# Sorting the edges of a graph layer by a scatter through DRAM in place of permutation products

## Chip, cores, metric

One core of one Trainium2 chip. The metric is the device time of one execution in microseconds (us); the kernel before takes 2326.83 us (median of 3 runs, 2326.06 to 2328.2).

## What is computed

Four graph layers, each `x = x + layer(relu(layernorm(x)))`, on `x` of 128 batches x 64 nodes x 256 features, all in float32. Layer 0 is a two-product network with batch norms around a normalised adjacency matrix; layer 1 works in the eigenvectors of the graph's Laplacian; layer 2 (the third) is two graph convolutions followed by LSTMs over windows of nodes; layer 3 (the fourth) is attention along 512 edges:

```
# layer 2, the convolutions
h = relu(einsum('ts,bsh->bth', adj, x @ Wg0 + bg0))
h = relu(einsum('ts,bsh->bth', adj, h @ Wg1 + bg1))
# ... LSTMs over windows of 1, 2, 3 and 4 nodes

# layer 3, E = 512 edges from src[e] to dst[e]
Xq, Xv = H @ W_lin.T, H @ W_val.T            # split into 4 heads
e = einsum('behd,hd->beh', leaky_relu(Xq[:, src] + Xq[:, dst], 0.2), a)
e = e + log(A0[src, dst] + 1e-8)
attn = softmax of e over the edges of the same src
Y = segment_sum(attn * Xv[:, dst], src)
out = Y @ W_out.T
```

Layer 3 is a sum over edges, so the edges may be taken in any order. The kernel sorts them by `src`, so that edges of one source stand side by side.

## The kernel before

The node features are kept in SBUF as 16 blocks `X[0..15]` of 512 rows (8 batches). TensorE (PE) does the products, VectorE (DVE) and ScalarE (ACT) take results out of PSUM, SyncE (SP) issues all DMAs, GpSimd (POOL) makes a few constants and otherwise does nothing. A float32 product of 128x512 is two entries of about 0.43 us each in the trace.

**The convolutions of layer 2** (`layer2`, L2088) run over the 16 blocks. `block(i)` (L2115) issues, in this order: the product with the first weights (`ps<-a,w`, four 128x512 products), taken out by DVE as `g`; the second mixing by the adjacency matrix of the block before (`features(i - 1)`, `ps<-BDA,y`), taken out by ACT into `big`; the first mixing of the block after (`mixed(i + 1)`, `ps<-BDA,h`), taken out as `a`, half by DVE and half by ACT; the product with the second weights (`pt<-w,g`), taken out by DVE in two halves as `y`; and the layer norm of block `i + 2` (`normed`), on DVE (`n_st`, `n_mv`, `n_v`, `n_r`, `n_m`) and ACT (`n_y`, `h`), with a DMA of `X[i + 2]` to DRAM (`xs<-X`). The LSTMs (`windows`, L2145) follow; their weights are loaded over blocks of `X` that are no longer needed, and their first inputs (`ls_tx`) are prepared ahead of time on DVE.

**The edge tables** of layer 3 (`edges`, L2332) are built inside layer 2, at the head of `block(2)`. Three small DMAs bring `src` and `dst` as columns (`ed_ci`, L2341: edge 128 c + p on partition p) and `src` as a row on all partitions (`ed_cmp`, L2342); POOL makes the index rows `ed_J`, `ed_C`, `ed_P` (L2348). With `key = src * 512 + e`, the place of an edge is the number of smaller keys: for each of four columns of edges DVE compares the row of all keys with 128 keys (`ed_cmp`) and sums (`ed_rank`). Then, for each column, DVE writes a 128x512 matrix with a one at each edge's place (`ed_perm`), and PE multiplies it with `src` and with `dst`: eight products `pe<-ed_perm,ed_col` into two PSUM banks. DVE copies the two sorted rows out (`ed_s`). Everything else follows from these two rows: the one-hot matrices of the ends `OS` and `OD` (again in buffers named `ed_perm`), their sum `ed_S`, their transposes `ed_OST` and `ed_ODT` (eight PE transposes `pe<-ident,ed_perm`), the marks of edges that continue a source (`ed_cont`, `ed_contr`), and the logarithm of the edge weights (`ed_log`: products `pe<-ed_perm,A` and `pe<-ed_cmp,ones`, and a Ln on ACT, which loads another function table). The buffers named `ed_` that are not used later lie in a pool `l3e`, which is given back when the tables are done.

**The order of instructions.** In layer 2 a scheduler of the framework orders the instructions of each engine by their dependences; each engine works through its list strictly in order. `nc.hold(nc.mark())` around `edges` puts each of its PE, DVE and ACT operations behind the last one issued so far on the same engine; where behind it, the scheduler decides. The trace attributes all PE, DVE and ACT operations to a helper's line, L799, so they are told apart here by the names of their tiles.

Of the kernel before, what the change touches and what calls it, by code (L numbers as in the profile page):

```python
# [8 lines left out]
F32 = mybir.dt.float32  # L9
I32 = mybir.dt.int32  # L10
AF = mybir.ActivationFunctionType
ALU = mybir.AluOpType
# [1453 lines left out]
class Kernel:  # L1466
# [621 lines left out]
    def layer2(self, pool, psum, ps2, ps0):  # L2088

        nc, o = self.nc, self.o  # L2090
        W0, W1, b1, N0 = self.tables2
        hs, as_, ys = {}, {}, {}

        def normed(i):
            if i < NB:
                hs[i] = self.norm(pool, i)
                nc.sync.dma_start(self.spilled(i), self.X[i][:])

        def mixed(i):
            if i < NB:  # L2100
                a = as_[i] = pool.tile([P, 2, BT], F32, name="a")
                self.mix(psum, hs.pop(i), self.BDA, lambda dc, p: self.move(a[:, dc, :], p[:]))

        def features(i):
            v = self.nodes(i // 4)
            b = 8 * (i % 4)
            self.mix(psum, ys.pop(i), self.BDA, lambda dc, p: self.act(
                v[:, dc, :, b:b + 8].rearrange("p n b -> p b n"), p[:].rearrange("p (b n) -> p b n", n=N), AF.Relu))

        def begin():  # L2110
            normed(0)
            mixed(0)
            normed(1)

        def block(i):  # L2115
            if i == 2:
                with ExitStack() as ce:
                    epool = ce.enter_context(self.tc.tile_pool(name="l3e", bufs=1, side="right"))
                    nc.hold(nc.mark())
                    self.edges(self.w3, epool, ps0)  # L2120
                    nc.hold()
            a = as_.pop(i)
            g = pool.tile([P, 2, BT], F32, name="g")
            for hc in range(2):
                p = psum.tile([P, BT], F32, name="ps")
                for kc in range(2):
                    self.mm(p[:], W0[:, kc, hc * P:(hc + 1) * P], a[:, kc, :], kc == 0, kc == 1)
                o.tt(g[:, hc, :].rearrange("p (b n) -> p b n", n=N), p[:].rearrange("p (b n) -> p b n", n=N),
                     N0[:, hc, None, :].to_broadcast([P, BT // N, N]), ALU.max)
            if i:  # L2130
                features(i - 1)
            mixed(i + 1)
            y = ys[i] = pool.tile([P, TPB, D], F32, name="y")
            for jj in range(0, TPB, 2):
                p = ps2.tile([P, 2, D], F32, name="pt")
                for j in range(2):
                    for kc in range(2):
                        self.mm(p[:, j, :], g[:, kc, (jj + j) * P:(jj + j + 1) * P], W1[:, kc, :],
                                kc == 0, kc == 1)
                o.add(y[:, jj:jj + 2, :], p[:], b1[:, None, :].to_broadcast([P, 2, D]))  # L2140
            normed(i + 2)

        return [begin] + [lambda i=i: block(i) for i in range(NB)] + [lambda: features(NB - 1)]
# [188 lines left out]
    def edges(self, w, pool, psum):  # L2332


        nc, o, io = self.nc, self.o, self.io
        ci, cmp = pool.tile([P, 2, 4], I32, name="ed_ci"), pool.tile([P, E], F32, name="ed_cmp")
        ri = cmp[:].bitcast(I32)
        with nc.allow_non_contiguous_dma("a few values"):
            for x, n in enumerate(("src", "dst")):
                a = io["L3_gnn_" + n]  # L2340
                nc.sync.dma_start(ci[:, x, :], a.rearrange("(c p) -> p c", p=P))  # L2341
        nc.sync.dma_start(ri, io["L3_gnn_src"].partition_broadcast(P))  # L2342
        row, col = pool.tile([P, E], F32, name="ed_row"), pool.tile([P, 2, 4], F32, name="ed_col")
        o.copy(row[:], ri)
        o.copy(col[:], ci[:])
        J, C = pool.tile([P, E], F32, name="ed_J"), pool.tile([P, 4], F32, name="ed_C")
        Pm = pool.tile([P, 1], F32, name="ed_P")
        iota = lambda t, pat, m: nc.gpsimd.iota(t[:], pattern=pat, base=0, channel_multiplier=m,  # L2348
                                                allow_small_or_imprecise_dtypes=True)
        iota(J, [[1, E]], 0)  # L2350
        iota(C, [[P, 4]], 1)
        iota(Pm, [[0, 1]], 1)
        up = pool.tile([P, 1], F32, name="ed_up")
        o.ts(up[:], Pm[:], float(N), ALU.is_ge, -float(N), ALU.mult)
        o.add(Pm[:], Pm[:], up[:])

        o.stt(row[:], row[:], float(E), J[:], ALU.mult, ALU.add)
        key = pool.tile([P, 4], F32, name="ed_key")
        o.stt(key[:], col[:, 0, :], float(E), C[:], ALU.mult, ALU.add)
        rank = pool.tile([P, 4], F32, name="ed_rank")  # L2360
        ps = [psum.tile([P, E], F32, name="pe") for x in range(2)]
        for c in range(4):
            o.ts(cmp[:], row[:], key[:, c:c + 1], ALU.is_lt)
            o.red(rank[:, c:c + 1], cmp[:], ALU.add)
            perm = pool.tile([P, E], F32, name="ed_perm", bufs=2)
            o.ts(perm[:], J[:], rank[:, c:c + 1], ALU.is_equal)
            for x in range(2):
                self.mm(ps[x][:], col[:, x, c:c + 1].to_broadcast([P, P]), perm[:], c == 0, c == 3)
        srt = []
        for x in range(2):  # L2370
            s = pool.tile([P, E], F32, name=f"ed_s{x}")
            o.copy(s[:], ps[x][:])
            srt.append(s)
        self.OS, self.OD = (pool.tile([P, E], F32, name="ed_perm", bufs=2) for _ in range(2))
        self.S2 = w.tile([P, E], F32, name="ed_S2")
        o.ts(self.OS[:], srt[0][:], Pm[:], ALU.is_equal)
        o.ts(self.OD[:], srt[1][:], Pm[:], ALU.is_equal)
        o.add(self.S2[:], self.OS[:], self.OD[:])
        self.OST, self.ODT = (w.tile([P, 4, N], F32, name="ed_" + n) for n in ("OST", "ODT"))
        for a, y in ((self.OS, self.OST), (self.OD, self.ODT)):  # L2380
            p = psum.tile([P, 4, N], F32, name="pe")
            for c in range(4):
                nc.tensor.transpose(p[:, c, :], a[:N, c * P:(c + 1) * P], self.ident[:N, :N])
            o.copy(y[:], p[:])

        self.cont, self.contr = (w.tile([P, E], F32, name="ed_" + n) for n in ("cont", "contr"))
        nc.vector.memset(self.cont[:], 0.0)
        nc.vector.memset(self.contr[:], 0.0)
        o.tt(self.cont[:, 1:E], srt[0][:, 1:E], srt[0][:, 0:E - 1], ALU.is_equal)
        o.copy(self.contr[:, 0:E - 1], self.cont[:, 1:E])  # L2390

        p = psum.tile([P, E], F32, name="pe")
        self.mm(p[:N, :], self.A[:], self.OS[:N, :])
        ga = cmp[:N, :]
        o.mul(ga, p[:N, :], self.OD[:N, :])
        p = psum.tile([P, E], F32, name="pe")
        self.mm(p[0:1, :], self.ones[:N, 0:1], ga)
        self.logA = w.tile([1, E], F32, name="ed_log")
        eps = pool.tile([1, 1], F32, name="ed_eps")
        nc.vector.memset(eps[:], 1e-8)  # L2400
        self.act(self.logA[:], p[0:1, :], AF.Ln, bias=eps[:])

        ac = self.columns(pool, "ed_ac", io["L3_gnn_a"].rearrange("h d -> (h d)"))
        self.apad = w.tile([P, 2, P], F32, name="ed_apad")
        nc.vector.memset(self.apad[:], 0.0)
        for fc in range(2):
            for x in range(2):
                s = slice(64 * x, 64 * x + 64)
                o.ts(self.apad[s, fc, 64 + 2 * fc + x:64 + 2 * fc + x + 1], ac[s, fc:fc + 1], 0.8, ALU.mult)
# [321 lines left out]
    def run(self):  # L2731
        self.begin()
        dram = self.ctx.enter_context(self.tc.tile_pool(name="xs", bufs=1, space=bass.MemoryType.DRAM))
        self.xs = dram.tile([B * N, D], F32, name="xs")
        cx, pools = self.stage([(f"big{q}", 1) for q in range(NG)])
        with cx:
            self.big = [pool.tile([P, 2, 4 * BT], F32, name="big") for pool in pools]
            with ExitStack() as ex:
                self.consts1 = ex.enter_context(self.tc.tile_pool(name="l1c", bufs=1))
                self.eigenvectors()  # L2740
                self.layers12()
            self.windows()
        self.layer3()
# [43 lines left out]
```

## Time and profile before

| | |
|---|---|
| median of 3 runs | 2326.83 us |
| profiled execution, its own time | 2326.85 us |
| profiled execution, span from first to last instruction | 2325.1 us |
| granted TensorE clock, mean | 0.997 |
| PE busy | 2283.6 us (98%) |
| DVE busy | 1629.3 us (70%) |
| ACT busy | 1139.5 us (49%) |
| POOL busy | 3.0 us |
| layer 2's 16 blocks, PE | 504.6 to 680.6 us of the span |
| edge tables, DVE | 513.3 to 536.2 us of the span |

The profile is of one execution. "Busy" is the time in which an engine had an instruction under way; matmuls are pipelined, so a busy PE is not one at its peak. The timeline gives, for each group of like instructions in order, its start and length; the start of the next group less its own start is the PE time that it took. Of several products in a row each entry overlaps the next.

### The profile page before, as it was taken

To read this page: it belongs to the slowest core of one execution; us is meant where nothing else is said; L and a number is where in the kernel's file an instruction comes from. 1 tells how busy PE (TensorE), PEld (TensorE's weight loads), DVE (VectorE), ACT (ScalarE), POOL (GpSimd) and SP (SyncE) were. 2 spreads that over 40 slices of the span, in tenths; PEclk is the share of its full clock that TensorE was granted. 3 is DMA by queue.
4 is the path that set the end of the run, shared out by engine and by line. 5 is a ranking of instruction groups with operands and counts; after the bars stand their busy time and mean duration, and the time that the engine had idled before them with its cause. 6 is when DMAs were issued, how large, how long until landed. Compare 5 with 4: busy or idle time off the path is not lost.

```text
span 2325.1 us, 32725 instructions
## 1 busy us (share of the span) xinstructions
PE 2283.6 (98%) x12169; PEld 1633.1 (70%) x12169; DVE 1629.3 (70%) x4054; ACT 1139.5 (49%) x2483; POOL 3.0 (0%) x26
## 2 busy tenths in 40 slices
PE   7999998999999999999999999999999999999999
PEld 4554445676777788888999998888885544554544
DVE  8887676888447777666767676559756686766667
ACT  5765865754436654433444444336435544444321
POOL 0000000000000000000000000000000000000000
PEclk9999999999999999999999999999999999999999
DMA  5000211230000000001000002000010000000001
GB/s 171 1 1 26 65 56 30 71 83 19 1 37 0 1 19 1 1 1 37 1 1 1 1 1 73 1 1 17 1 46 28 1 5 15 15 19 14 14 24 46
DMA packets 61065, 54.81 MB, mean 24 GB/s; under 512 B 15203, under 2 KB 58724, under 8 KB 60900
## 3 DMA queue, kind: packets, MB, share of 16 engines
q1 hardware_dynamic: 60900, 52.66, 7.4%
q8 instruction: 97, 1.59, 0.3%
q14 instruction: 68, 0.56, 0.1%
HBM read 35.86 MB, written 16.78 MB: 23 GB/s over the span
## 4 chain that ended last, share of the span: by engine, by line
PE 79%; DVE 3%; issue 1%; ACT 1%; DMA 0%; SPq 0%; ACTq 0%; DVEq 0%
PE ps L799 69%; PE acc L799 5%; PE pt L799 4%; PE pe L799 1%; PE y L799 1%; DVE aw L799 1%; DVE X L799 1%; DVE sm_m L799 0%; DVE XV L799 0%; ACT ls_g L799 0%; ACT h L799 0%; DVE ls_g L799 0%; ACT big L799 0%; DVE ls_t L799 0%; DVE sm_e L799 0%
## 5 line engine op out<-in xcount | busy, mean ns | idle before, releaser
L799 ACT ACTIVATE ls_g<-ls_g,ls_b 128x512 f32<-128x512 f32 (+4 forms) x472 | 243.1, 565 | 151.4 <-DVE ls_g L799 149.6
L799 ACT ACTIVATE ls_g<-ps,ls_b 128x256 f32<-128x256 f32 (+3 forms) x268 | 115.5, 470 | 330.9 <-PE ps L799 327.7
L799 PE MATMUL ps<-z,w 128*128 128x512 f32 x512 | 254.9, 621 | 0.9 <-ACT z L799 0.9
L799 PE MATMUL ps<-big,X 128*128 128x176 f32 (+3 forms) x848 | 212.7, 366 | 0.1
L799 DVE TENSOR_TENSOR ls_g<-ls_z,ps 128x512 f32<-128x512 f32 (+5 forms) x256 | 146.8, 579 | 91.9 <-PE ps L799 90.4
L799 DVE TENSOR_TENSOR aw<-at,ed_OST 128x1024 f32<-128x1024 f32 x128 | 149.9, 1219 | 83.0 <-PE ps L799 82.8
L799 PE MATMUL ps<-ls_tx,X 128*128 128x160 f32 (+2 forms) x960 | 206.8, 326 | 0.6 <-ACT ls_g L799 0.6
L799 PE MATMUL ps<-X,X 128*128 128x160 f32 (+1 forms) x896 | 199.1, 306 | 0.0
L799 PE MATMUL ps<-X,ls_w 128*128 128x256 f32 x640 | 190.5, 379 | 0.0
L799 PEld LDWEIGHTS ps<-ls_tx,X 128*128 128x128 f32 x960 | 161.8, 190 | 15.1 <-DVE X L799 4.8
L799 PEld LDWEIGHTS ps<-big,X 128*128 128x128 f32 x848 | 145.9, 190 | 29.7 <-issue 19.4
L799 DVE TENSOR_TENSOR X<-ls_g 128x1024 f32<-128x1024 f32 (+2 forms) x108 | 117.4, 1087 | 49.9 <-ACT ls_g L799 49.8
L799 ACT ACTIVATE r<-ps 128x512 f32<-128x512 f32 x256 | 131.6, 614 | 41.5 <-PE ps L799 41.4
L799 PEld LDWEIGHTS ps<-X,X 128*128 128x128 f32 x896 | 148.4, 190 | 0.0
L799 PE MATMUL ps<-X,ls_s 128*128 128x256 f32 x480 | 142.3, 379 | 0.0
L799 PEld LDWEIGHTS ps<-z,w 128*128 128x128 f32 x512 | 87.2, 190 | 69.0 <-issue 60.2
L799 PE MATMUL ps<-ls_tx,ls_s 128*128 128x256 f32 x464 | 134.8, 379 | 0.0
L799 PE MATMUL ps<-ed_S,Q 64*128 64x512 f32 x512 | 132.9, 618 | 1.4 <-DVE hT L799 0.7
L799 PE MATMUL ps<-ls_tx,ls_w 128*128 128x256 f32 x464 | 133.2, 380 | 0.0
L799 PEld LDWEIGHTS ps<-X,ls_w 128*128 128x128 f32 x640 | 121.4, 190 | 16.8 <-DVE X L799 0.3
L799 PE MATMUL ps<-big,ls_w 128*128 128x256 f32 x464 | 131.9, 379 | 0.7 <-ACT ls_z L799 0.7
L799 PE MATMUL ps<-aw,ed_ODT 128*64 128x512 f32 x512 | 117.3, 595 | 0.1
(545 smaller groups left out, 4019.0 us busy)
## 6 DMA issues: line engine op xcount, KB each, us to landing
X<-in_x_dram SPq DMA_DIRECT2D x32, 512.0 KB
xs<-X SPq DMA_DIRECT2D x16, 512.0 KB
X<-xs SPq DMA_DIRECT2D x16, 512.0 KB
out_dram<-X SPq DMA_DIRECT2D x31, 256.0 KB
X<-in_L_gnn_Wih_t_dram SPq DMA_DIRECT2D x4, 512.0 KB
ls_w<-in_L_gnn_Wih_t_dram SPq DMA_DIRECT2D x4, 512.0 KB
ls_w<-in_L_gnn_Whh_t_dram SPq DMA_DIRECT2D x4, 512.0 KB
w<-in_L_gnn_W_t_dram SPq DMA_DIRECT2D x2, 512.0 KB
```

What stands on the lines that cost most here:

```text
L799: i = method(*a, **kw)
```

## The change

The sort is done by DMA. DVE turns the four rank columns into integers (`ed_at`). POOL then issues, for each column and each end, an indirect DMA that writes 128 integers of `ed_ci` to the places `ed_at` of a DRAM tensor `ends[x]` (8 DMAs), and two plain DMAs that bring `ends[0]` and `ends[1]` back as rows on all 128 partitions. The permutation matrices, their eight PE products and their two PSUM buffers are gone; DVE's copies `ed_s` convert the integers of the returned rows to float32. The work is cut in two: the first part (loads, ranks, DMAs) is issued at the head of `block(4)`, the second (`sorted`, from the two rows to the tables) at the head of `block(9)`, each with its own `hold`. The pool `l3e` stays open from one to the other.

```diff
         def block(i):
-            if i == 2:
-                with ExitStack() as ce:
-                    epool = ce.enter_context(self.tc.tile_pool(name="l3e", bufs=1, side="right"))
-                    nc.hold(nc.mark())
-                    self.edges(self.w3, epool, ps0)
-                    nc.hold()
+            if i == 4:
+                self.ce = ExitStack()
+                epool = self.ce.enter_context(self.tc.tile_pool(name="l3e", bufs=1, side="right"))
+                nc.hold(nc.mark())
+                self.tables3 = self.edges(self.w3, epool, ps0)
+                nc.hold()
+            if i == 9:
+                nc.hold(nc.mark())
+                self.tables3()
+                nc.hold()
+                self.ce.close()
...
         rank = pool.tile([P, 4], F32, name="ed_rank")
-        ps = [psum.tile([P, E], F32, name="pe") for x in range(2)]
+        at = pool.tile([P, 4], I32, name="ed_at")
         for c in range(4):
             o.ts(cmp[:], row[:], key[:, c:c + 1], ALU.is_lt)
             o.red(rank[:, c:c + 1], cmp[:], ALU.add)
-            perm = pool.tile([P, E], F32, name="ed_perm", bufs=2)
-            o.ts(perm[:], J[:], rank[:, c:c + 1], ALU.is_equal)
-            for x in range(2):
-                self.mm(ps[x][:], col[:, x, c:c + 1].to_broadcast([P, P]), perm[:], c == 0, c == 3)
+        o.copy(at[:], rank[:])
+
         srt = []
         for x in range(2):
-            s = pool.tile([P, E], F32, name=f"ed_s{x}")
-            o.copy(s[:], ps[x][:])
-            srt.append(s)
+            for c in range(4):
+                nc.gpsimd.indirect_dma_start(self.ends[x][:], bass.IndirectOffsetOnAxis(ap=at[:, c:c + 1], axis=0),
+                                             ci[:, x, c:c + 1], None)
+            s = pool.tile([P, E], F32, name="ed_perm", bufs=2)[:].bitcast(I32)
+            nc.gpsimd.dma_start(s, self.ends[x][:].rearrange("e o -> (o e)").partition_broadcast(P))
+            srt.append((pool.tile([P, E], F32, name=f"ed_s{x}"), s))
+        return lambda: self.sorted(w, pool, psum, Pm, cmp, *srt)
+
+    def sorted(self, w, pool, psum, Pm, cmp, *srt):
+
+        nc, o, io = self.nc, self.o, self.io
+        for x, s in srt:
+            o.copy(x[:], s)
+        srt = [x for x, s in srt]
         self.OS, self.OD = (pool.tile([P, E], F32, name="ed_perm", bufs=2) for _ in range(2))
...
         self.xs = dram.tile([B * N, D], F32, name="xs")
+        self.ends = [dram.tile([E, 1], I32, name=f"ends{x}") for x in range(2)]
```

## The prediction, on record before the changed kernel ran

> **What bounds the kernel now.** First the head of the page, then the chain of waits over the stretch in which the edge tables are built, because a share over the whole span does not say who sets the pace there.
>
> ```profile
> span 2325.1 us, 32725 instructions
> PE 2283.6 (98%) x12169; PEld 1633.1 (70%) x12169; DVE 1629.3 (70%) x4054; ACT 1139.5 (49%) x2483; POOL 3.0 (0%) x26
> ```
>
> The chain of waits from 500 to 600 us (start, length, what):
>
> ```profile
> 513.55 7.00 PE ps L799 x40
> 520.55 3.46 PE pt L799 x16
> 524.01 6.87 PE pe L799 x16
> 530.87 0.86 PE ps L799 x2
> 531.73 0.39 PE pe L799 x4
> 532.12 1.91 PE ps L799 x4
> 534.04 1.39 PE pe L799 x6
> 535.43 1.50 PE ps L799 x6
> 536.93 0.95 PE pe L799 x2
> 537.88 3.32 PE ps L799 x28
> 541.20 3.46 PE pt L799 x16
> 544.65 7.00 PE ps L799 x40
> 551.66 3.46 PE pt L799 x16
> 555.11 7.00 PE ps L799 x40
> ```
>
> The chain is PE and nothing else. A block of layer 2 costs 7.00 + 3.46 = 10.46 us, the same beside the table work and far from it. The `pe` entries are the tables' own products, put between: 6.87 us for the sixteen entries of the permutation products, then 0.39, 1.39 and 0.95 us. Now the other engines, by windows (PE busy, PEld, DVE, ACT, POOL, clock, DMA share, GB/s):
>
> ```profile
> 528.00:532.00 4.00, 4.00 (x13) 1.65 (x11) 4.00 (x22) 1.59 (x4) 0.00 (x0) 1.00 0.45 131
> 590.00:600.00 10.00, 10.00 (x56) 7.90 (x55) 4.72 (x15) 4.73 (x8) 0.00 (x0) 1.00 0.01 2
> ```
>
> DVE is full during the table work and half empty at 590 us; PE is full in both. So the permutation products are real time on the engine that sets the end, and DVE work here is not.
>
> **What the Trainium skill says.** "DMA: Bandwidth & Descriptors", section "Anatomy of one DMA — SWDGE (gpsimd) path", prices a DMA issued from GpSimd at about 2.0 us fixed plus bytes/436e3 us, most of the fixed part being the wait until the last byte has landed. The same page, "Latency and other measured facts", gives about 1 us to the first byte for such a DMA and 0.6 us from SyncE. The trace before has no DMA from POOL at all; its nearest rows are the two 16 KB loads at the start, from SP:
>
> ```profile
> 0.74 0.58 SPq L1509 DMA_DIRECT2D A<-in_adj_dram  x1
> 1.38 0.58 SPq L1510 DMA_DIRECT2D AT<-in_adj_t_dram  x1
> 2.88 0.21 DVE L799 TENSOR_REDUCE f_a_rs<-A 64x1 f32<-64x64 f32 x1 [1.23 <-DMA A<-in_adj_dram]
> 3.62 0.21 DVE L799 TENSOR_REDUCE f_a_cs<-AT 64x1 f32<-64x64 f32 x1 [0.53 <-DMA AT<-in_adj_t_dram]
> ```
>
> From issue to first use 2.88 - 0.74 = 2.14 us and 3.62 - 1.38 = 2.24 us, which agrees with the fixed price. "SBUF — State Buffer", its box on the "DVE blocks DMA" trap, adds that DVE operations in a two-port mode keep GpSimd from writing descriptors: a DMA of 620 ns took 3100 ns there. No run here shows that yet.
>
> **The change, part by part.**
>
> *Removed from PE:* eight products, sixteen entries, 6.87 us from the chain (523.84 to 530.71 in the timeline). No stall is hidden in it: 16 x 0.43 = 6.9. All of it lies on the path.
>
> *Moved on PE:* the eight transposes, the product with `A` and the one with `ones`, from block 2 to the start of block 9. Before they took 0.39 + 0.39 + 1.00 + 0.95 = 2.73 us, and cut the neighbours into pieces: the `ps` entries around them sum to 0.86 + 1.91 + 1.50 + 3.32 = 7.59 us instead of 7.00, so 0.59. Check: 544.65 - 524.01 = 20.64 = 10.46 + 6.87 + 2.73 + 0.59, to rounding. In the changed instruction order the transposes stand together, then one 128x512 product, `A`, one product, `ones`, and the block goes on; `ps<-BDA,y`, split before (1.99 us in place of 1.78), stays whole, a gain of 0.2. Against that, `ones` now has one product of 0.86 us ahead of it to cover DVE's `ed_cmp` (683 ns and its signals, after the product with `A` has drained). I estimate 0 to 1 us of PE wait and take 0.3. Net on PE: 6.87 + 0.2 - 0.3 = 6.8 us.
>
> *DVE:* four `ed_perm` operations go (371 to 477 ns, 1.8 us) and two PSUM copies of 0.68 us become two conversions in SBUF (nearest row: the 0.41 us cast of `ed_row`); one small copy of 0.16 us is added. Some 2.2 us less, and the rest is spread over blocks 1 to 9. Taken as nothing, because PE never waited in the fuller version. *ACT:* one of two 1.28 us table loads goes, as no `n_y` follows `ed_log` any more; nothing, ACT being half idle. The six `ls_tx` subtractions move from block 4 to block 9, since they use memory of `l3e`; their first reader stands at 681.5 us, more than 70 us later: nothing. *SP:* the same DMAs in the same order; the new ones pass none of them.
>
> *Added: a chain of DMAs on POOL.* Ten DMAs go into POOL's queue, empty after the three index rows. Each scatter waits for the scatter two before it (same DRAM tensor), and each read-back for its tensor's last scatter. Two chains run interleaved, so five links deep if POOL issues fast, ten if each DMA in effect waits for the one before. A link costs at least 2.2 us (the SP rows), 2.6 with the 0.4 us that the skill puts on GpSimd's first byte; computing 128 destinations in software makes it more. I take 3.5 us, an estimate that leaves 0.9 us for it; the upper bound adds the lock's 3.1 - 0.6 = 2.5 us: 6.0. So the chain takes 5 x 3.5 = 17.5 us likely, 5 x 2.2 = 11 us at least, 10 x 3.5 = 35 us if serial, 10 x 6.0 = 60 us at worst.
>
> *The added wait.* DVE's first `ed_s` copy waits for the first row read back. Behind it in DVE's list are the second `y` of block 5 and everything after; PE's `ps<-BDA,y` in block 6 waits for that `y`. The window: the blocks start on PE at 523.84 (block 2), 534.30, 544.76, 555.22 (block 5). `ed_at` follows block 2's second `g`, about 4 us after that block's start (517.12 against 513.38 for block 1), with 0.6 us for the operation: about 528.5. The first `ed_s` follows block 5's first `y`, 9.1 us after the start (522.49 against 513.38), plus 0.6: 564.9. Window 36.4 us. PE still has a second-weights half and block 6's first products, so it starves only some 3 us later: 39 us.
>
> **Sum:** 2326.85 us of the profiled execution (span 2325.1 and 1.75 around it; equal to the median of 2326.83 to 0.02) - 6.8 = 2320.05 us. From block 10 on all engines have the same order as before, and PE fills the boundary to the LSTMs without a gap, so the shift should reach the end.
>
> **Rivals.** *The main case* (gain kept): 0.77, time 2318.8 to 2321.8.
>
> *The chain is somewhat late*, 41 to 46 us of DMA: PE waits 2 to 7 us in block 6, the gain shrinks to 5 to 0 us, time 2322 to 2327. For: the price of computed destinations is not in the trace, and the first use of that path may be dearer. Against: it needs links of 8 us and more in two chains, or over 4 us in one. 0.09.
>
> *The wait exceeds what was removed*, at DVE's first `ed_s`. At 39 + 6.8 = 46 us of chain the change breaks even; from there each microsecond is one lost. At the worst, 60 us: 2326.85 - 6.8 + 21 = 2341 us. It decides at links of 4.6 us in one serial chain, or 9.2 us in two. For: the lock of the shared port and descriptors for single integers. Against: DVE's operations at 530 to 565 us are under 0.7 us each and mostly read PSUM, so that ten locks in a row are unlikely. 0.08.
>
> *The products were not what PE waited for*: if DVE had set the pace at 513 to 536 us, the removal would bring only DVE's 2.2 us: 2324.6. Against it stands the chain without a DVE piece. 0.04; and 0.02 for a larger gain.
>
> **How the numbers follow.** A measurement of this kernel can tell about 0.2%, 4.65 us, from no change. Faster than 2322.2 us: the main case, the larger gain, and 0.02 of the late one: 0.81. Slower than 2331.5 us: 0.07 of the 0.08 above. Within: the other 0.07 of the late case, the 2324.6 us case, and 0.01: 0.12. The time is that of the main case, 2320.1. The range, 2318.7 to 2324.7, takes in the main case, the case without PE's wait and the nearer half of the late one: 0.77 + 0.04 + 0.04 = 0.85.
>
> **What would show it.** Right: no `pe<-ed_perm,ed_col`; block starts on PE 10.46 us apart from block 2 to 9; the last scatter landed before 555 us; no idle time of DVE before `ed_s`; block 9 longer by about 3.2 us; the first `ps<-big,X` at about 673.8 us instead of 680.6. Wrong: DVE idle before `ed_s` until a DMA, with PE idle in block 6, or an LSTM start that moved less than PE's removed time.

## The result, and the profile after

The changed kernel takes 2322.21 us (median of 20 runs), the kernel before, run beside it on the same chip, 2328.57 us (20 runs). The ratio is 0.9974, with a 95% interval of 0.9967 to 0.9981: 6.1 us less (4.4 to 7.7). Forecast were 2320.1 us and 6.8 us less.

The head of the page, and its line for the new DMA queue (packets, MB, share):

```profile
span 2316.7 us, 32710 instructions
PE 2274.4 (98%) x12153; PEld 1628.0 (70%) x12153; DVE 1626.7 (70%) x4051; ACT 1138.3 (49%) x2482; POOL 12.0 (1%) x36
q0 software_dynamic: 416, 0.53, 0.1%
```

PE has 16 entries fewer, DVE three operations, ACT one (the table load); POOL has ten DMAs more and is still idle for 99% of the span. The chain of waits over the same stretch as before, and on to the new place of the tables:

```profile
513.42 7.00 PE ps L799 x40
520.42 3.46 PE pt L799 x16
523.88 7.00 PE ps L799 x40
530.88 3.46 PE pt L799 x16
...
593.64 3.46 PE pt L799 x16
597.10 0.64 PE pe L799 x8
597.74 1.06 PE ps L799 x2
598.79 1.00 PE pe L799 x2
599.79 1.06 PE ps L799 x2
600.85 0.95 PE pe L799 x2
601.80 5.49 PE ps L799 x36
```

Where 6.87 us of `pe` stood, the next block follows at once, and the blocks from 513 to 597 us are 10.46 us each. What is left of the tables on PE stands at 597 us in three pieces. The chain holds nothing but PE: no piece of DMA, POOL or DVE has come in. The two windows shown of before (PE busy, PEld, DVE, ACT, POOL, clock, DMA share, GB/s):

```profile
528.00:532.00 4.00, 4.00 (x32) 3.86 (x32) 4.00 (x22) 2.92 (x6) 2.35 (x3) 1.00 0.01 0
590.00:600.00 10.00, 10.00 (x62) 7.67 (x61) 4.90 (x17) 5.27 (x9) 0.00 (x0) 1.00 0.01 2
```

From 528 to 532 us PE is as full as it was, but with 32 entries of a block in place of 13 that were mostly permutation products. DVE is full as before, and POOL now works beside it.

The executions of one kernel differ by several microseconds in their first 500 us, before anything that the change touches. So the traces are compared by a distance: from the first product of block 1 (`ps<-a,w`) to the first product of the LSTMs (`ps<-big,X`), both on PE. It holds all that was removed, moved or added:

| kernel | block 1 | LSTMs | distance, us | less than before |
|---|---|---|---|---|
| before | 513.38 | 680.62 | 167.24 | |
| after | 513.25 | 673.49 | 160.24 | 7.00 |

The two profiled spans differ by 8.4 us. The other 1.4 us come from elsewhere: at the start of layer 3 the execution shown of before ran at a granted clock of 0.50 from 1745.4 to 1752.2 us, and one group of eight products took 3.78 us there; after has a clock of 1.00 and 1.99 us for the same group. Of the experiments' traces, some show the long form (x1: 3.78 us) and some the short one (x3: 1.99 us), with or without the change. It is no part of the change.

The DMAs on POOL, and their reader (timelines of POOL and DVE; start, length, idle time before and what ended it):

```profile
528.43 1.14 POOL L2375 DMA_INDIRECT ends<-ed_ci,ed_at  x1 [155.62 <-DVE n_r L799]
529.87 0.99 POOL L2375 DMA_INDIRECT ends<-ed_ci,ed_at  x1 [0.30 <-issue]
531.78 0.96 POOL L2375 DMA_INDIRECT ends<-ed_ci,ed_at  x1 [0.92 <-DMA ends<-ed_ci,ed_at]
...
541.31 0.58 POOL L2378 DMA_DIRECT2D ed_perm<-ends  x1 [0.25 <-issue]
544.28 0.56 POOL L2378 DMA_DIRECT2D ed_perm<-ends  x1 [2.40 <-DMA ends<-ed_ci,ed_at]
```

```profile
565.76 0.16 DVE L799 SCALAR_TENSOR_TENSOR n_m<-n_mv,n_r 128x4 f32<-128x4 f32 x1
565.85 0.42 DVE L799 CAST ed_s<-ed_perm 128x512 f32<-128x512 int32 x1
566.18 0.68 DVE L799 TENSOR_TENSOR y<-pt,w_b 128x512 f32<-128x512 f32 x1
```

The trace has the landing of four of the eight scatters: 2.5 to 4.3 us from issue (median 3.2 us). A read-back takes 4.0 us. The first and third scatter go to different places of one tensor, and the third waits for the first. The second row has landed at 544.28 + 4.0 = 548.3 us. DVE comes to `ed_s` at 565.85 us, without idle time in front of it: 17.5 us to spare.

### The profile page after: what moved, and what is told of

Same layout as the page of the kernel before. It is cut to its first block, busy times and chain, and to the rows that moved or that the text cites. A ratio compares the mean times of both kernels' runs of the same rounds, so it can differ in the third digit from the quotient of the medians.

```text
span 2316.7 us, 32710 instructions
## 1 busy us (share of the span) xinstructions
PE 2274.4 (98%) x12153; PEld 1628.0 (70%) x12153; DVE 1626.7 (70%) x4051; ACT 1138.3 (49%) x2482; POOL 12.0 (1%) x36
## 4 chain that ended last, share of the span: by engine, by line
PE 79%; DVE 3%; ACT 1%; issue 1%; DMA 0%; SPq 0%; ACTq 0%; DVEq 0%
PE ps L799 69%; PE acc L799 5%; PE pt L799 4%; PE y L799 1%; PE pe L799 1%; DVE aw L799 1%; DVE X L799 1%; DVE sm_m L799 0%; DVE XV L799 0%; ACT ls_g L799 0%; ACT h L799 0%; DVE ls_g L799 0%; DMA X<-in_L_gnn_Wih_t_dram 0%; ACT big L799 0%; DVE ls_t L799 0%
## 5 line engine op out<-in xcount | busy, mean ns | idle before, releaser
L799 ACT ACTIVATE big<-ps 128x512 f32<-128x512 f32 x96 | 69.2, 751 | 102.9 <-PE ps L799 101.6
```

Source lines behind the costliest of these rows:

```text
L799: i = method(*a, **kw)
```

## Experiments

Two theories stood against each other at first. **Theory:** the gain is the PE time of the removed products, and the DMA chain is free because five blocks of other work stand between its issue and its reader. **Rivals:** the gain comes from the new places of the two parts; or the DMA chain costs something that hides part of the gain. Each run is read by the distance above and by its ratio to the kernel before (with a 95% interval). Where an expectation names the start of the LSTMs in us of one execution (x1, x3, x5, x6), it is read as a distance too: 673.5 us stands for 160.24, 680.6 for 167.24.

### The products kept, the new places used

```diff
-            nc.gpsimd.indirect_dma_start(self.ends[x][:], ...)   # 8, and the two read-backs
     def sorted(...):
+            o.ts(perm[:], J[:], rank[:, c:c + 1], ALU.is_equal)   # 4
+                self.mm(ps[x][:], col[:, x, c:c + 1].to_broadcast([P, P]), perm[:], c == 0, c == 3)   # 8
+            o.copy(s[:], ps[x][:])   # 2
```

> The eight permutation products, their four one-hot matrices and the two PSUM copies are kept as before, but the work is cut and placed as in the change (ranks at block 4, everything else at block 9); no scatter. Theory 1 (the gain is the PE time of the eight products): the LSTMs start on PE at 680.6 us (+-0.5), as before, and the time is that of before within 2 us. Rival A (the gain comes from moving and spreading the table work, products or not): LSTM start at 673.5 us, time 6 us below before.

Ratio 1.0005 (0.9997 to 1.0013); distance 167.24 us, that of before to the last digit. In the chain of waits the 6.87 us are back, at the new place:

```profile
597.08 3.46 PE pt L799 x16
600.54 6.87 PE pe L799 x16
607.41 0.86 PE ps L799 x2
```

So placing the parts apart brings nothing by itself; all 7.00 us go with the products.

### No DMA chain at all

```diff
-            nc.gpsimd.indirect_dma_start(self.ends[x][:], ...)   # 8
-            nc.gpsimd.dma_start(s, self.ends[x][:]...)
+            nc.sync.dma_start(s, io["L3_gnn_" + ("src", "dst")[x]].partition_broadcast(P))
```

> The changed kernel without the ten POOL DMAs: the two rows are loaded from src and dst as they are, by SP, so the edges stay unsorted. Theory 1 (the chain of DMAs is fully hidden): LSTM start at 673.5 us (+-0.3), time equal to the changed kernel's, 6 us below before. Rival B (the DMA chain costs something beside the path, through the shared port or DVE slowed): start up to 2 us earlier, 671.5 to 673.2.

Ratio 0.9976 (0.9968 to 0.9985); distance 160.23 us against 160.24 with the chain. The ten DMAs cost PE nothing in this stretch (0.01 us).

### The wait laid open: the same chain, less cover

Three kernels bring the reader nearer to the DMAs. In the first both parts stand together:

```diff
             if i == 4:
-                self.tables3 = self.edges(self.w3, epool, ps0)
-            if i == 9:
-                self.tables3()
+                self.edges(self.w3, epool, ps0)()
```

> The scatters are used, but both parts stand together at the fifth block: ranks, DMAs and tables in one piece, so nothing is put between the ten DMAs and their reader. In the instruction order DVE's first ed_s stands right behind block 3's `a`, and PE's transposes at the start of block 4. Theory (the products' 6.87 us are saved, and the DMA chain costs nothing only because the tables stand five blocks further back): the rows land some 20 us after ed_at, while DVE comes to ed_s some 13 us after it, so DVE and then PE wait, PE for about 5 to 7 us; from block 1's first product to the first product of the LSTMs about 165 to 167 us (before 167.24, after 160.24), the time 0.998 to 1.0005 of the kernel before. Rival (the chain would be hidden anyway, as PE has enough other work there): 160 to 161 us and 0.997.

Ratio 1.0033 (1.0017 to 1.0048), slower than before the change; distance 171.88 us. The loss against the change, 11.64 us, is far over the 5 to 7 us expected. PE's timeline in block 4:

```profile
547.92 3.62 PE L799 MATMUL pt<-w,g 128*128 128x256 f32 x16
554.81 1.08 PE L799 MATMUL pe<-ident,ed_perm 64*128 64x64 f32 x8 [3.27 <-DVE ed_perm L799]
555.82 2.07 PE L799 MATMUL ps<-a,w 128*128 128x512 f32 x2
557.94 1.96 PE L799 MATMUL pe<-ed_perm,A 64*64 64x512 f32 x2
559.83 3.78 PE L799 MATMUL ps<-a,w 128*128 128x512 f32 x4
563.54 1.86 PE L799 MATMUL pe<-ed_cmp,ones 64*1 64x512 f32 x2
```

and the windows over it:

```profile
551.70:555.10 3.40, 0.29 (x4) 0.29 (x4) 1.59 (x5) 0.28 (x1) 0.00 (x0) 1.00 0.35 83
555.10:568.70 13.60, 13.56 (x27) 4.91 (x26) 8.75 (x25) 0.68 (x1) 0.00 (x0) 0.50 0.00 1
```

The wait itself is 3.27 us. Behind it the granted clock is 0.50 for 13.6 us, and each group takes about double what it takes at full clock (timelines of x4 and x10): the transposes 1.08 us for 0.71, two entries of `ps<-a,w` 2.07 for 1.1, four 3.78 for 1.98. "Busy" does not show it: PE is at 13.56 of 13.60 us there. Block 4 takes 23.60 us, where the next kernel has 13.64: 9.96 us more, of which 3.3 are standing still and about 6.7 half speed. The other 1.69 us lie in front of the LSTMs, where PE waited 1.52 us for ACT's `big`; why, the runs do not say.

The control has the joined order without the DMAs:

```diff
             # on x2_joined
-            nc.gpsimd.indirect_dma_start(self.ends[x][:], ...)   # 8
-            nc.gpsimd.dma_start(s, self.ends[x][:]...)
+            nc.sync.dma_start(s, io["L3_gnn_" + ("src", "dst")[x]].partition_broadcast(P))
```

> x2_joined without its DMA chain: both parts stand together at the fifth block, and the two rows are loaded by SP from the inputs early, so that nothing is waited for (the edges then stand in the order given, not sorted). Theory (x2's loss of 11.64 us against the change is DMA wait and what the wait sets off, PE's half clock after it): without the wait PE never stands still in block 4 and its clock stays at 1.00, so 160.2 to 162 us from block 1's first product to the LSTMs (x2 171.88), up to 1.7 us of that being the boundary to the LSTMs, where x2 waited 1.52 us for ACT; the ratio 0.9975 to 0.9985. Rival (it is the joined order itself that is bad): 168 us or more, and no better than the kernel before.

Ratio 0.9963 (0.9944 to 0.9981); distance 160.23 us; no idle time of PE in the blocks. The order does no harm; the 11.65 us between the two kernels are the wait and what it set off.

The other two keep the parts apart, but bring the second forward:

```diff
-            if i == 9:
+            if i == 7:      # in the other kernel: 6
                 nc.hold(nc.mark())
                 self.tables3()
```

> Only the place of the second part is changed: tables behind the eighth block instead of the tenth. DVE's first ed_s then stands behind block 3's second `y`, near the time at which the rows land. Theory (20 us of DMA chain against what stands ahead of ed_s): DVE waits 0 to 3 us at ed_s, PE has more than that in stock, so 160.2 to 161 us from block 1's first product to the LSTMs. Rival (any wait of DVE is passed on to PE in full): 162 to 163 us.

> The change with its second part behind the seventh block in place of the tenth. DVE's first ed_s stands behind block 3's `a`, some 5 us ahead of the landing of the rows. Theory: PE has 3 us in stock, so it stands still for about 2 to 5 us; each microsecond of it costs one, and if the clock falls after it as in x2, some 6 us more: 162 to 165 us from block 1's first product to the LSTMs at full clock, 168 to 172 at half clock behind the wait (after 160.24, block 7 161.42, x2 171.88). Rival (PE has other work in stock): 160.3 us.

At block 7 DVE waits, and the chain of waits now runs through the DMA (start, length, what):

```profile
551.38 4.44 DMA ed_perm<-ends
555.82 0.02 issue
555.84 0.43 DVE ed_s L799
556.27 0.60 DVE g L799
...
558.79 1.16 PE ps L799 x8
```

DVE waits 2.04 us, and PE's distance is 161.42 us, 1.18 us longer than after. At block 6 DVE waits 3.11 + 1.10 = 4.2 us, and the distance is 163.33 us, 3.09 us longer. PE's entries with a wait there, and a window over two of them:

```profile
550.00 0.71 PE L799 MATMUL ps<-BDA,y 128*128 128x128 f32 x4 [0.45 <-DVE y L799]
551.53 1.60 PE L799 MATMUL ps<-BDA,y 128*128 128x128 f32 x12 [0.82 <-DVE y L799]
555.05 1.16 PE L799 MATMUL ps<-BDA,h 128*128 128x128 f32 x8 [0.90 <-DVE g L799]
```

```profile
550.00:555.00 5.00, 3.33 (x24) 2.90 (x24) 5.00 (x18) 2.21 (x3) 0.00 (x0) 1.00 0.02 3
```

In these two executions the wait reaches PE in short pieces, the clock stays at 1.00, and it costs about one microsecond less than DVE waited. So with the tables two blocks earlier than in the change PE begins to pay, and three blocks earlier it pays in earnest. The times of these single runs (2328.04 us at block 7, 2323.32 at block 6) say nothing here: block 1 starts at 520.22 us in the first and at 514.57 in the second.

### A chain three times as long

```diff
+                for again in range(3):
                     nc.gpsimd.indirect_dma_start(self.ends[x][:], ...)
```

> Every scatter of the changed kernel is issued three times, 24 in all. From the trace of the changed kernel 8 scatters take 15.9 us and a read-back 4.0 us, so 24 take 47.6 us: the rows land at about 577 and 580 us, and DVE's first ed_s stands at 565.9. Theory 1 with the slack of 3 us that the prediction gives PE: PE waits 9 us for the second y of block 5 and 1 to 3 us more for the g of block 6; LSTM start at 684 us (682 to 687), time 3 to 6 us above before. Rival C (PE has more cover than that, or the DMAs of repeated scatters overlap): start at 673.5 to 680 us, time still below before.

Ratio 0.9998 (0.9989 to 1.0007); distance 164.58 us, so 2.66 us of the gain are left. The LSTMs start at 684.55 us, inside the 682 to 687 foreseen, but by luck: block 1 began 6.7 us later in this execution than in that of after. And this was not the wait foreseen. The 24 scatters were issued 1.6 us apart on average, not 2, the rows came when DVE was there, and yet DVE stood still before that (6.48 us), at an operation that waits for PE alone. A second execution:

> The same kernel as x5_scatter_three_times, looked at once more, for the holds of DVE (6.48 us at 573.13) and ACT (3.34 us at 574.66, from an unknown queue) that no semaphore of the program explains. If they belong to the 24 scatters on POOL, they come at the same places again, with block 1 to the LSTMs at about 164.6 us; if they were a chance of that one execution, they are elsewhere or gone, and about 160.3 to 163 us is left.

Distance 164.04 us, and the holds again (timelines of DVE and ACT):

```profile
567.11 0.69 DVE L799 COPY a<-ps 128x512 f32<-128x512 f32 x1 [7.27 <-PE pt L799]
570.75 0.42 DVE L799 CAST ed_s<-ed_perm 128x512 f32<-128x512 int32 x1
```

```profile
565.64 1.04 ACT L799 ACTIVATE big<-ps 128x512 f32<-128x512 f32 x1 [1.80 <-remote]
```

DVE idles for 7.27 us in front of `a`, until 1.7 us after POOL's last scatter has ended (565.4 us; in the first execution until 573.13 us, 0.1 us after it), and then comes to `ed_s` without a wait. The kernel after idles for 1.68 us in front of the same `a`, so 4.8 and 5.6 us are new. The trace names the end of PE's `pt` as what ended it; `a` takes a product that was done 5 us earlier (at 562.1 us). ACT (1.80 us, `remote`) and PE itself (0.31 us inside `pt`, at 565.3 us) paused too, with no instruction of the program named as releaser, so this is no wait of DVE alone. The loss of 3.8 to 4.3 us comes with these DMAs, since nothing else was changed, but not through `ed_s`; of the 4.3 us some 1.7 are half speed (an estimate: in the first execution the clock was 0.50 for 3.4 us behind PE's stand). Whether the number of indirect DMAs does it was asked with 24 that nobody reads:

```diff
             # on x3_no_scatter
+            nc.gpsimd.indirect_dma_start(self.junk[8 * k + 4 * x + c][:], ...)   # 24, one tensor each
```

> x3_no_scatter (rows loaded unsorted by SP, nothing waits for POOL) with 24 indirect DMAs of 128 values put on POOL behind ed_at, each into a place of its own in DRAM that nobody reads. So no instruction of DVE, ACT or PE has anything to wait for from them. First reading of the holds in x5 (a row of indirect DMAs issued without a pause keeps the other engines from going on, whatever waits for them): the 24 are issued 1.26 us apart for some 30 us, DVE and ACT show idle times of 2.5 to 7 us that no semaphore of theirs explains, and PE loses 2 to 5 us, 162 to 165 us from block 1's first product to the LSTMs. Second reading (the holds come from the waits for ed_s and its rows): 160.2 us, no such idle times.

```profile
557.30 0.69 DVE L799 COPY a<-ps 128x512 f32<-128x512 f32 x1 [1.74 <-PE ps L799]
559.86 0.69 DVE L799 TENSOR_TENSOR X<-X,X 128x512 f32<-128x512 f32 x1 [1.86 <-ACT h L799]
```

POOL issued them 1.26 us apart from 534.78 to 565.2 us, without a pause; DVE's longest idle time in that stretch is the 1.86 us shown, with a releaser that explains it, and the distance is 160.23 us. So in this one execution neither the number nor the density of indirect DMAs held the others. What differs is that the scatters of x5 write the same two tensors over and over, wait for one another and are read back; which of these it is stays open. The last kernel of this group tested nothing:

```diff
             # on x3_no_scatter, behind ed_at
+        for k in range(48):
+            iota(idle, [[1, E]], 0)
```

> As x8_unread_scatters, but in place of 24 indirect DMAs 48 index rows of 128x512 (0.56 us each in the trace of after) written by POOL into a tile that nobody reads, some 27 us behind ed_at. If POOL's being busy holds the others, the idle times come here too and 162 us or more are found; if it is the indirect DMAs, 160.2 us and none.

Its 48 index rows depended on nothing and ran from 373 to 403 us, ahead of the blocks in question (distance 160.23 us).

### More of the same: no table work on PE

If PE's time in the chain is the whole price, the 3.18 us of table work that is left should go the same way. `OST` and `ODT` are compared by DVE from sorted columns read back from DRAM, and the entries of `A` are gathered by four indirect DMAs and scattered by rank, like the ends:

```diff
+            nc.gpsimd.indirect_dma_start(val[:, c:c + 1], None, io["adj"]..., where[:, c:c + 1])   # 4
+            nc.gpsimd.indirect_dma_start(self.vals[:], at[:, c:c + 1], val[:, c:c + 1], None)      # 4
-            nc.tensor.transpose(p[:, c, :], a[:N, c * P:(c + 1) * P], self.ident[:N, :N])           # 8
+            o.tt(y[:], J[:, None, 0:N]..., fcol[:, x, :, None]..., ALU.is_equal)                    # 2
-        self.mm(p[:N, :], self.A[:], self.OS[:N, :])
-        self.mm(p[0:1, :], self.ones[:N, 0:1], ga)
```

> The changed kernel with the rest of the table work taken off PE: the transposed one-hot matrices are written by DVE from sorted columns that two more POOL DMAs read back, and the edge weights are gathered from adj by four indirect DMAs, scattered by rank like the ends (four more) and read back as a row for the logarithm. Theory 1 (each us of PE in this stretch is one us of time, DMAs are free while the window holds): LSTM start 3.2 us before the changed kernel's, at 670.3 us; time 10 us below before (ratio 0.9957). Rival D (the longer chain, about 12 scatters, or the 17 DMAs on POOL miss the window): start at 672 us or later.

Ratio 0.9967 (0.9956 to 0.9979); distance 158.14 us, 2.10 less than after, where 3.18 had been removed. (By the trace POOL has 21 DMAs here, not 17.) The 1.08 us were lost in block 3, which took 11.55 us, again by DVE idling (2.56 us before a `y` whose product was done) while POOL was at its twelve scatters. The next kernel packs the three numbers of an edge into one row of 12 bytes, so that four scatters and ten DMAs do:

```diff
             # on x6_tables_without_pe
-            nc.gpsimd.indirect_dma_start(self.ends[x][:], ..., ci[:, x, c:c + 1], None)    # 8
-            nc.gpsimd.indirect_dma_start(self.vals[:], ..., val[:, c:c + 1], None)         # 4
+            nc.gpsimd.indirect_dma_start(self.ends[:], ..., ci[:, c, :], None)             # 4, ends is [E, 3]
+        nc.gpsimd.dma_start(rows[:].rearrange("p e x -> p (e x)"), self.ends[:]...)        # both rows and the values
+            nc.gpsimd.dma_start(cols[:], self.ends[:].rearrange("(c p) x -> p c x", p=P))
```

> As x6_tables_without_pe (no table work on PE at all: A's entries gathered by four indirect DMAs, OST and ODT compared from sorted columns), but the three numbers of an edge (source, end, value of A) are scattered as one row of 12 bytes: four scatters, one broadcast of the rows and one of the columns, in all ten DMAs on POOL in place of the twenty of x6. Theory (each of PE's instructions removed from the chain is a gain of its own length, and the DMA chain is hidden): PE loses the last 3.18 us of table work, so 157.1 us from block 1's first product to the LSTMs (after 160.24, x6 158.14), if the hold of DVE that cost x6 1.08 us came with the number of DMAs on POOL; 158.1 us if it did not. The ratio to the kernel before 0.996 (after: 0.9974).

Ratio 0.9961 (0.9947 to 0.9976); distance 157.05 us, 3.19 us less than after and 10.19 less than before. The chain of waits over the blocks has no `pe` at all:

```profile
587.84 3.46 PE pt L799 x16
591.30 7.00 PE ps L799 x40
598.30 3.46 PE pt L799 x16
601.76 7.00 PE ps L799 x40
```

By the trace this is the fastest version; the intervals of the ratios of x7 and of the change overlap, so the times alone do not separate the two. That the hold of x6 is gone does not show that the number of DMAs made it: x7 also scatters into one tensor in place of three, and x8 speaks against the number.

## Why the prediction was right

**The removed products.** Forecast were 6.87 us, all on the path. They are what x1 puts back. Right.

**The moved table work.** Forecast: +0.2 us for an unsplit `ps<-BDA,y`, -0.3 us for a wait of PE before the product with `ones`. The chain after has that product at 600.85 us right behind its neighbour, with no wait; the table part takes 3.18 us where it took 3.31. So +0.13 and 0, a net of 7.00 in place of 6.8 us. The interleaved block product does cover DVE's `ed_cmp`.

**What was costed at nothing.** DVE lost 2.6 us of work and ACT 1.2 us (2.2 and 1.28 foreseen), and PE's distance shows none of it. The moved `ls_tx` operations and SP's list show nothing either.

**The DMA chain.** Forecast: a link of 3.5 us, five deep, 17.5 us. Measured: 528.43 to 548.3 us, 19.9 us. The second chain starts 1.44 us behind the first, which the sum left out, and takes 18.4 us, 3.7 us a link. The low bound of 2.2 us, from SP's rows at the start, held: the shortest landing recorded of the change took 2.5 us. The two interleaved chains were right: in POOL's timeline a scatter waits for the one two before it. "DMA: Bandwidth & Descriptors", section "Anatomy of one DMA — SWDGE (gpsimd) path", has a formula that gives, as an estimate, 2.0 us for a DMA of 512 bytes and 2.6 us for a read-back of 256 KB; the trace has a median of 3.2 us for the scatters and 4.0 us for the read-back. The two differ, and the measurement decides: 1.2 and 1.4 us were missing. In x7, where each of the four scatters had landed before the next was issued, they took 2.1 to 3.0 us (median 2.1), close to that estimate; whether it is the second chain beside it that makes the scatters of the change slower was not tested. The lock that "SBUF — State Buffer", its box on the "DVE blocks DMA" trap, warns of did not show: with DVE busy for 4.00 of 4.00 us, the three scatters issued there took 0.96 to 1.14 us of POOL each. (The 620 and 3100 ns stand further down on that page, in "A bandwidth-pool intuition that's wrong (but worth ruling out)".)

**The window.** Forecast 528.5 to 564.9 us; found 528.43 to 565.85. Of 37.4 us the chain uses 19.9. So the rival of a late chain, and that of a wait larger than what was removed, were far off; the second needed 46 us of chain.

**The rivals' mechanism.** That such a wait can turn the change into a loss is real: x2 is 4.64 us of distance behind the kernel before. But two numbers of its price were off, though neither touched the forecast. PE's stock was put at 3 us; at blocks 7 and 6 it was about 1 us (2.04 us of waiting cost 1.18, 4.2 cost 3.09). And "each microsecond is one lost" misses what a long stand of PE did in x2, where 3.27 us of it cost 10 us, two thirds of that by the clock.

**The signs.** All came: no product `pe<-ed_perm,ed_col`, blocks 2 to 9 at 10.46 us, the last scatter landed at 544.0 us (named: before 555), no idle time of DVE before `ed_s`, block 9 longer by 3.18 us (3.2), the LSTMs at 673.5 us (673.8). The time, 2322.21 us, is 2.1 us above the forecast, inside the range of 2318.7 to 2324.7 but 0.4 us above that of the main case; the forecast stood on an execution of 2326.85 us, and the runs of before beside it have a median of 2328.57, 1.7 us higher.

## What to carry to other kernels

Where one engine fills the chain of waits, count its instructions: those taken away were worth their own time here (7.00 us in the change, 3.19 more in x7). Work handed to DMA was free in both, its landing lying ahead of its reader's turn in the list. That the landing is early enough is needed, but it did not suffice everywhere: x5 and x6 lost 1.1 to 4.3 us with no wait at the reader. Split issue and use, and keep some microseconds in hand: the split is what made this change a gain, since the same DMAs read at once made a loss. When PE is made to wait in one piece, look at the granted clock behind the wait, not only at its length.

## What was not expected of the hardware

The clock: behind a stand of 3.27 us in x2 PE ran at 0.50 of its clock for 13.6 us. Half speed came elsewhere too, for 3.4 us in x5 and for 6.8 us in before (windows of before, then of x5):

```profile
1742.00:1745.40 3.40, 2.62 (x13) 1.56 (x13) 2.51 (x4) 2.77 (x6) 0.00 (x0) 1.00 0.75 242
1745.40:1752.20 6.80, 5.73 (x15) 4.03 (x14) 4.93 (x17) 2.71 (x5) 0.00 (x0) 0.50 0.53 183
```

```profile
575.70:579.00 3.30, 3.30 (x5) 1.35 (x4) 1.62 (x7) 1.51 (x4) 0.00 (x0) 0.50 0.55 111
```

These are one, two and four times 3.4 us. "TensorE: Matmul & The Clock Gate", section "Part 1: The HAM clock gate (the "warmup" mystery)", describes such a halving, after an idle window of about 3.4 us whose start is not tied to the program, and ended by about 3.4 us of sustained work. The step of 3.4 us, and that the halving differs between executions, agree with the runs: 1.53 us of standing in x5 was followed by half speed, 1.64 us in its second execution by a clock of 1.00. What does not agree is the idle window: in the 3.4 us ahead of the halving PE stood still for 3.1 us in x2, but only for 1.8 in x5 and 0.8 in before. Nor did sustained work end it in x2 within 3.4 us: PE had instructions under way for 13.56 of the 13.60 us. What is counted as idle or as work, the runs do not show.

The holds: in x5 (both executions) and x6 DVE idled 2.6 to 7.3 us, and in x5 ACT too, at operations that took products already done, while POOL was at chained scatters or just behind them. In x5 they came again at about the same place. They cost PE 1.1 to 4.3 us. With eight chained scatters (the change) or 24 unconnected ones there was none. The cause is open.
